# A hybrid two-layer kernel on Trainium2: the maxima of causal attention computed for two heads at a time on 64 rows each

## The chip, the cores and the metric

The kernel runs on one core of one Trainium2 chip. A time is the device time of one execution in microseconds (us); "before" is the median of three runs. Next to it stands one execution recorded by the hardware profiler. Times inside that execution are counted from the start of its span. The engines are TensorE (PE in the profile; its weight loads are PEld), VectorE (DVE), ScalarE (ACT), GpSimd (POOL) and SyncE (SP), which here only issues DMAs.

## The reference, cut to what matters

The reference is two layers of several sublayers each, with a residual sum around each: a complex-valued scan (`sublayer_a`), a routed feed-forward, a second attention-like sublayer and the same feed-forward, then a long convolution (`sublayer_c`), a ternary feed-forward, causal self-attention (`sublayer_d`) and the ternary feed-forward again. The change touches only the causal attention, on x of shape (2, 2048, 256), with 16 heads of 16 features:

```python
q, k, v = (proj(Wq), proj(Wk), proj(Wv))        # (B, heads, S, 16)
q = _apply_rope(q, cos, sin)
k = _apply_rope(k, cos, sin)
scores = jnp.einsum('bhqd,bhkd->bhqk', q, k) * scale      # scale = 1/4
scores = jnp.where(causal[None, None], scores, -jnp.inf)
attn = jax.nn.softmax(scores, axis=-1)
out = jnp.einsum('bhqk,bhkd->bhqd', attn, v)
out = out.transpose(0, 2, 1, 3).reshape(B, S, 256)
return jnp.einsum('bsd,ed->bse', out, Wo)
```

The softmax subtracts the maximum of each row of scores before the exponential.

## The kernel before

`tile_hybrid_kernel` calls the sublayers one after the other. `sublayer_d` first calls `attention_inputs`, which writes q, k (each as a high and a low part[...]) and v to device memory (`qd`, `kd`, `vd`). Then it works in units. A unit is one batch `b`, one group `g` of four heads and one chunk `ch` of 512 queries; it needs the keys of chunks 0 to `ch`. There are 2 x 4 x 4 = 32 units, four of them (`ch` 0 to 3) in each of the eight groups.

`load_unit` (L1446 and after) fills a tile `d_kt` (six of them in turn) and a tile `d_qt` (three in turn) for a unit. `stack` (L1439) does it with four DMAs for each: the features of a head lie four times over on 64 partitions, as high and low parts in the orders that make a product of 64 rows the sum of all four high-low combinations. Rows 64 and 65 of `d_kt` are ones. Rows 64 and 65 of `d_qt` are set to zero by GpSimd (L1459) and later take the negative row maxima as a high and a low part, and all other rows to 127 are zero. So a product over 128 partitions gives the scores before the maxima are known, and the scores less the maxima afterwards.

`maxima` (L1463) makes the row maxima of a unit. For each head `hh`, block `i` of 128 queries and key chunk `j` it makes a product into a `ps_m` buffer (L1472; three buffers of 128 x 512) and reduces it on VectorE: with `tensor_reduce` (L1482), or, on the diagonal chunk, with an added mask row (L1477). The results stand in `d_part`; at the end they are reduced to `d_mx` (L1485), transposed by TensorE into the single buffer `ps_x` (L1489), split (L1491, L1492) and sent into rows 64 and 65 of `d_qt` by two DMAs on ScalarE's queue. It is a generator that yields after each product.

`attend` (L1497) runs over the key tiles `kt` of 128 keys. For each of four heads it makes the transposed scores into a `ps_e` buffer (L1515; three buffers); on the diagonal it adds the causal mask with a second product (L1520: `d_mask` times `d_identr`). ScalarE takes the exponential into a `d_p` buffer (L1522; six buffers), and then `filler` may let the next unit's `maxima` go on. When the four heads of a key tile are issued, the value products of the key tile before it follow (`values`, L1503), into four strips of 32 partitions of `ps_o`; `v` has ones appended, so that the sums of the softmax come out too. At the end ScalarE copies `ps_o` to `d_on` (L1531), and the sums are turned over by three DMAs of GpSimd's queue around a reciprocal on VectorE (L1535). `normalize` and `project` (L1549) finish the unit one step later: products with `Wo` into `ps_x` (L1554), added to `self.x` by VectorE (L1559).

In the loop at the end of `sublayer_d` step `n` runs `attend` of unit `n` with `maxima` of unit `n + 1` in between, spread over the first 70% of the key tiles, and issues the loads of unit `n + 2`:

```python
filler(1.0)
if late is not None:
    project(*late)
late = (unit, on)
```

TensorE's instructions run in the order in which this code writes them (`tc.manual_schedule(engines={PE})`). The order on the other engines is decided when the kernel is compiled, by a scheduler that works with its own estimate of times; on the chip each engine keeps that order.

Of the kernel before, what the change touches and what calls it, by code (L numbers as in the profile page):

```python
# [16 lines left out]
F32 = mybir.dt.float32  # L17
# [46 lines left out]
class Kernel:  # L64
# [1320 lines left out]
    def sublayer_d(self):  # L1385
# [5 lines left out]

        tc, nc = self.tc, self.nc
# [3 lines left out]
        with ExitStack() as c:  # L1396
# [8 lines left out]
            mask, identr = r32(kp, [P, P], "d_mask"), r32(kp, [P, P], "d_identr")  # L1405
            V.tensor_copy(mask, maskf)
            V.tensor_copy(identr, self.ident)
# [18 lines left out]
            qring = [r32(qp, [P, 4, CH], f"d_qt{j}") for j in range(QR)]  # L1426
            for t in qring:
                G.memset(flat(t, HR, P), 0.0)
# [3 lines left out]
            sp = c.enter_context(tc.tile_pool(name="d_s", bufs=6))  # L1432
            pm = c.enter_context(tc.tile_pool(name="d_pm", bufs=3, space=PSUM))
            pe = c.enter_context(tc.tile_pool(name="d_pe", bufs=3, space=PSUM))
            po = c.enter_context(tc.tile_pool(name="d_po", bufs=1, space=PSUM))
            px = c.enter_context(tc.tile_pool(name="d_px", bufs=1, space=PSUM))
            wo = self.load(kp, "D_WoP", pat="(k p) n -> p k n", p=P)

            def stack(t, src, b, g, blk, order):  # L1439
                for r, half in enumerate(order):  # L1440
# [3 lines left out]
                    )  # L1444

            def load_unit(b, g, ch):  # L1446
# [8 lines left out]
                stack(kring[(n * 4 + ch) % KR], kd, b, g, ch, (0, 0, 1, 1))  # L1455
                q = qring[(n * 4 + ch) % QR]
                stack(q, qd, b, g, ch, (0, 1, 0, 1))
                if n * 4 + ch >= QR:
                    G.memset(flat(q, HR, ROWS), 0.0)  # L1459
                ks = [kring[(n * 4 + j) % KR] for j in range(ch + 1)]  # L1460
                return b, g, ch, q, ks, vring[n % 2]

            def maxima(unit):  # L1463

                b, g, ch, q, ks, ve = unit
                part = new(tp, [P, 4, 4, 4], "d_part")
                for hh in range(4):
                    for i in range(4):
                        for j in range(ch + 1):
                            w = (i + 1) * P if j == ch else CH  # L1470
                            ps = new(pm, [P, CH], "ps_m")
                            nc.tensor.matmul(  # L1472
                                ps[:, :w], q[:, hh, i * P : (i + 1) * P], ks[j][:, hh, :w], start=True, stop=True
                            )
                            if j == ch:
                                junk = new(jp, [P, CH], "d_junk")
                                V.tensor_tensor_reduce(  # L1477
                                    out=junk[:, :w], in0=ps[:, :w], in1=late_keys[:, CH - w :], scale=1.0,
# [16 lines left out]
                yield  # L1495

            def attend(unit, o, filler):  # L1497
                b, g, ch, q, ks, ve = unit
                nk = 4 * ch + 4

                def values(kt, q0, prs):
# [196 lines left out]
```

## Time and profile before

| | us |
|---|---|
| median of three runs | 13912.62 (13908.2 to 13919.0) |
| the profiled execution | 13913.98 |
| its span, first to last instruction | 13912.3 |
| busy in the span: DVE | 10663.1 (77%) |
| busy in the span: ACT | 9306.1 (67%) |
| busy in the span: PE | 5521.0 (40%) |
| units of `sublayer_d` in the span | 12322 to 13756 |
| in this stretch: PE, DVE, ACT busy | 1254.9, 762.0, 624.4 |
| in this stretch: granted TensorE clock | 0.96 |

The busy shares of the whole span are those of the scan, which takes about the first 10000 us and keeps TensorE mostly idle. A row of a group gives the line, the engine, the operation and the tiles (written first), then the count, the time in which at least one of them ran, the mean duration in ns, and the idle time of the engine just before them with what ended it. Matmul durations overlap: the pace is in the distance from one start to the next. In the timeline, a bracket at the end of a row gives the idle time before it and what ended it.

### The profile page before, as it was taken

To read this page: it belongs to the slowest core of one execution; us is meant where nothing else is said; L and a number is where in the kernel's file an instruction comes from. 1 tells how busy PE (TensorE), PEld (TensorE's weight loads), DVE (VectorE), ACT (ScalarE), POOL (GpSimd) and SP (SyncE) were. 2 spreads that over 40 slices of the span, in tenths; PEclk is the share of its full clock that TensorE was granted. 3 is DMA by queue.
4 is the path that set the end of the run, shared out by engine and by line. 5 is a ranking of instruction groups with operands and counts; after the bars stand their busy time and mean duration, and the time that the engine had idled before them with its cause. 6 is when DMAs were issued, how large, how long until landed. Compare 5 with 4: busy or idle time off the path is not lost. (4 is left out here: it accounts for less than half of the span.)

```text
span 13912.3 us, 263001 instructions
## 1 busy us (share of the span) xinstructions
PE 5521.0 (40%) x66344; PEld 3798.1 (27%) x66344; DVE 10663.1 (77%) x65491; ACT 9306.1 (67%) x45234; POOL 432.4 (3%) x496
## 2 busy tenths in 40 slices
PE   4222222222222222222222222222289766778888
PEld 2111111111111111111111111111255444544445
DVE  6888888888888888888888888888857655555555
ACT  3777777777777777777777777777626366434444
POOL 0000000000000000000000000000000000131110
PEclk7555555555555555555555555555579778889999
DMA  3000000000000000000000000000000144242210
GB/s 80 14 15 16 17 14 17 14 17 17 14 17 14 17 17 14 17 14 17 17 14 17 14 17 17 14 17 14 14 13 1 41 123 132 62 94 35 33 32 19
DMA packets 334776, 382.28 MB, mean 27 GB/s; under 512 B 207074, under 2 KB 247081, under 8 KB 332212
## 3 DMA queue, kind: packets, MB, share of 16 engines
q1 hardware_dynamic: 289204, 281.11, 8.8%
q10 hardware_dynamic: 29184, 49.82, 1.3%
q0 software_dynamic: 14848, 34.36, 0.9%
q8 instruction: 533, 8.73, 0.3%
q14 instruction: 1007, 8.25, 0.2%
HBM read 307.96 MB, written 52.46 MB: 26 GB/s over the span
## 5 line engine op out<-in xcount | busy, mean ns | idle before, releaser
L410 PE MATMUL hc<-hs,mean 128*32 128x2 f32 x16384 | 588.2, 203 | 7116.8 <-DVE hs L480 7052.2
L410 PEld LDWEIGHTS hc<-hs,mean 128*32 128x32 f32 x16384 | 412.7, 140 | 7328.8 <-DVE hs L480 7263.8
L475 DVE TENSOR_TENSOR p<-p,ir 128x64 f32<-128x64 f32 x4096 | 739.0, 222 | 1065.4 <-ACT ir L463 1065.4
L459 ACT ACTIVATE lm<-m 128x64 f32<-128x64 f32 x2048 | 466.2, 228 | 1216.3 <-DVE m L451 1216.3
L493 PE MATMUL yps<-cs,hist 128*64 128x8 f32 x8192 | 1225.0, 259 | 13.0 <-DVE hs L480 13.0
L391 ACT ACTIVATE bx<-dx,tc 128x64 f32<-128x64 f32 x4098 | 1169.4, 332 | 0.1
L1522 ACT ACTIVATE d_p<-ps_e 128x512 f32<-128x512 f32 (+3 forms) x1280 | 599.4, 537 | 756.1 <-PE ps_o L1503 534.2
L493 PEld LDWEIGHTS yps<-cs,hist 128*64 128x64 f32 x8192 | 1033.2, 218 | 45.1 <-DVE hs L480 13.4
L418 ACT ACTIVATE sq<-hc 128x2 f32<-128x2 f32 x2048 | 353.2, 172 | 794.0 <-PE hc L410 794.0
L480 DVE CUSTOM_DVE_ANT_0 hist<-p,sg 128x64 f32<-128x64 f32 x4096 | 764.5, 224 | 22.5 <-ACT rm L470 4.2
L442 DVE TENSOR_TENSOR p<-p,fac 128x64 f32<-128x64 f32 x4096 | 741.6, 222 | 8.9 <-DVE p L437 6.6
L477 DVE SCALAR_TENSOR_TENSOR p<-e,p 128x64 f32<-128x64 f32 x4096 | 740.6, 222 | 9.9 <-ACT sg L469 7.8
L444 DVE TENSOR_TENSOR p<-p,bx 128x64 f32<-128x64 f32 x4096 | 727.5, 219 | 2.5
L439 ACT ACTIVATE fac<-ngd,ci 128x64 f32<-128x64 f32 x2048 | 711.8, 348 | 1.0 <-DVE p L436 1.0
L436 DVE SCALAR_TENSOR_TENSOR p<-hist,ea 128x64 f32<-128x64 f32 x2048 | 461.1, 225 | 321.8 <-ACT ea L429 321.8
L429 ACT ACTIVATE ea<-ex 128x64 f32<-128x64 f32 x2048 | 524.3, 256 | 102.7 <-DVE ex L424 7.0
L1515 PE MATMUL ps_e<-d_qt,d_kt 128*128 128x512 f32 (+3 forms) x1280 | 558.1, 445 | 44.3 <-ACT d_p L1522 35.5
L472 ACT ACTIVATE ld<-e 128x64 f32<-128x64 f32 x2048 | 548.2, 268 | 0.0
L410 PE MATMUL hd<-hs,mean 128*32 128x2 f32 x16384 | 544.3, 193 | 0.0
L473 ACT ACTIVATE k<-rm 128x64 f32<-128x64 f32 x2048 | 544.1, 266 | 0.0
L1472 PE MATMUL ps_m<-d_kt,d_qt 128*128 128x512 f32 (+3 forms) x1280 | 499.9, 438 | 99.1 <-DVE d_part L1477 39.9
L1165 PE MATMUL ps_c<-toep,c_x 128*32 128x128 f32 x9216 | 407.5, 341 | 306.6 <-ACT toep L1114 304.9
(452 smaller groups left out, 22795.9 us busy)
## 6 DMA issues: line engine op xcount, KB each, us to landing
ng<-dtd SPq DMA_DIRECT2D x258, 256.0 KB, 3.7
dx<-dxd SPq DMA_DIRECT2D x258, 256.0 KB, 4.2
toep<-in_C_krev ACTq DMA_DIRECT2D x128, 312.0 KB, 4.7
toep<-in_C_krev SPq DMA_DIRECT2D x128, 312.0 KB, 4.7
d_kt<-d_kd SPq DMA_DIRECT2D x128, 128.0 KB, 4.1
d_qt<-d_qd SPq DMA_DIRECT2D x128, 128.0 KB, 3.8
y<-ys SPq DMA_DIRECT2D x512, 8.0 KB, 1.9
c_xd<-c_xs POOLq DMA_DIRECT2D x32, 256.0 KB, 4.5
```

The source lines that it names most:

```text
L391: A.activation(bx[o][:, k2], tg[j][2][:, k], AF.Identity, scale=tg[j][0][:, k2, k : k + 1], bias=0.0 if k2 else SMALL,)
L410: nc.tensor.matmul(out[r : r + 32], mean[:, r : r + 32], hs[i], start=True, stop=True)
L439: A.activation(fac, ngd, AF.Exp, scale=ci)
L442: V.tensor_tensor(p[:, k2], p[:, k2], fac, ALU.mult)
L444: V.tensor_tensor(p[:, k2], p[:, k2], bx[o][:, k2], ALU.add)
L472: A.activation(ld, e, AF.Ln, scale=-1.0, bias=1.0)
L475: V.tensor_tensor(p[:, k2], p[:, k2], ir, ALU.mult)
L477: V.scalar_tensor_tensor(p[:, k2], e, -1.0, p[:, k2], ALU.add, ALU.mult)
L480: V.tensor_tensor_reduce(out=hn[:, k2], in0=p[:, k2], in1=sg, scale=-1.0, scalar=0.0 if k2 else J * SMALL, op0=ALU.mult, op1=ALU.add, accu ...
L493: nc.tensor.matmul(yps[:, k, :], hist[g][:, k, k2], tg[g][3][:, k2, k], start=k2 == 0, stop=k2 == 1)
L1515: nc.tensor.matmul(s[:, q0:], ks[kt // 4][:, hh, kt % 4 * P : (kt % 4 + 1) * P], q[:, hh, q0:], start=True, stop=not diag,)
L1522: A.activation(pr[:, q0:], s[:, q0:], AF.Exp, scale=0.25)
```

## The change

The products for the maxima are made for two heads at a time. The even head uses rows 0 to 63 of `d_qt` and `d_kt`, as they are; the odd head uses rows 64 to 127 of new tiles `d_qq` (two in turn) and `d_kk` (five in turn), which a DMA inside SBUF copies from rows 0 to 63 of the odd heads. Each product thus takes 64 of TensorE's rows, and the two of a pair go to different rows and different `ps_m` buffers. `maxima` yields once per pair. The rows 64 and 65 of `d_qt` are no longer read before the maxima are in them, and the memset of them goes. The mask and the identity that adds it are bfloat16. The pool of `ps_x` goes; its users take a `ps_m` buffer, and there are four of these instead of three. There are eight `d_p` buffers instead of six.

```diff
@@ -1402,9 +1404,9 @@
             kp = c.enter_context(tc.tile_pool(name="d_k", bufs=1))
             maskf = new(kp, [P, P], "d_maskf")
             make_causal_mask(nc, maskf, MASKED)
-            mask, identr = r32(kp, [P, P], "d_mask"), r32(kp, [P, P], "d_identr")
+            mask, identb = (kp.tile([P, P], BF16, name=n, tag=n) for n in ("d_mask", "d_identb"))
             V.tensor_copy(mask, maskf)
-            V.tensor_copy(identr, self.ident)
+            V.tensor_copy(identb, self.ident)
 
             late_keys = new(kp, [P, CH], "d_late")
             G.memset(late_keys, 0.0)
@@ -1424,24 +1426,26 @@
             self.attention_inputs(qd, kd, vd)
             qp = c.enter_context(tc.tile_pool(name="d_q", bufs=1))
             qring = [r32(qp, [P, 4, CH], f"d_qt{j}") for j in range(QR)]
+            q2ring = [r32(qp, [P, 2, CH], f"d_qq{j}") for j in range(2)]
+            k2ring = [r32(qp, [P, 2, CH], f"d_kk{j}") for j in range(5)]
             for t in qring:
                 G.memset(flat(t, HR, P), 0.0)
             tp = c.enter_context(tc.tile_pool(name="d_t", bufs=2))
             jp = c.enter_context(tc.tile_pool(name="d_j", bufs=1))
             op = c.enter_context(tc.tile_pool(name="d_o", bufs=3))
-            sp = c.enter_context(tc.tile_pool(name="d_s", bufs=6))
-            pm = c.enter_context(tc.tile_pool(name="d_pm", bufs=3, space=PSUM))
+            sp = c.enter_context(tc.tile_pool(name="d_s", bufs=8))
+            pm = c.enter_context(tc.tile_pool(name="d_pm", bufs=4, space=PSUM))
             pe = c.enter_context(tc.tile_pool(name="d_pe", bufs=3, space=PSUM))
             po = c.enter_context(tc.tile_pool(name="d_po", bufs=1, space=PSUM))
-            px = c.enter_context(tc.tile_pool(name="d_px", bufs=1, space=PSUM))
             wo = self.load(kp, "D_WoP", pat="(k p) n -> p k n", p=P)
 
-            def stack(t, src, b, g, blk, order):
+            def stack(t, t2, src, b, g, blk, order):
                 for r, half in enumerate(order):
                     nc.sync.dma_start(
                         out=t[r * 16 : (r + 1) * 16].bitcast(F32),
                         in_=src[b, g * 4 : g * 4 + 4, half, :, blk * CH : (blk + 1) * CH].rearrange("h c t -> c h t"),
                     )
+                nc.sync.dma_start(out=t2[HR:P].bitcast(F32), in_=t[0:HR, 1::2].bitcast(F32))
 
             def load_unit(b, g, ch):
                 n = b * 4 + g
@@ -1452,40 +1456,41 @@
                             out=vring[n % 2][:, :, hh, 0:16],
                             in_=vd[b * S : (b + 1) * S, h * 16 : (h + 1) * 16].rearrange("(i p) e -> p i e", p=P),
                         )
-                stack(kring[(n * 4 + ch) % KR], kd, b, g, ch, (0, 0, 1, 1))
-                q = qring[(n * 4 + ch) % QR]
-                stack(q, qd, b, g, ch, (0, 1, 0, 1))
-                if n * 4 + ch >= QR:
-                    G.memset(flat(q, HR, ROWS), 0.0)
-                ks = [kring[(n * 4 + j) % KR] for j in range(ch + 1)]
-                return b, g, ch, q, ks, vring[n % 2]
+                u = n * 4 + ch
+                stack(kring[u % KR], k2ring[u % 5], kd, b, g, ch, (0, 0, 1, 1))
+                q, q2 = qring[u % QR], q2ring[u % 2]
+                stack(q, q2, qd, b, g, ch, (0, 1, 0, 1))
+                ks, k2s = ([ring[(n * 4 + j) % len(ring)] for j in range(ch + 1)] for ring in (kring, k2ring))
+                return b, g, ch, q, ks, vring[n % 2], q2, k2s
 
             def maxima(unit):
 
-                b, g, ch, q, ks, ve = unit
+                b, g, ch, q, ks, ve, q2, k2s = unit
                 part = new(tp, [P, 4, 4, 4], "d_part")
-                for hh in range(4):
+                for hp in range(2):
                     for i in range(4):
                         for j in range(ch + 1):
                             w = (i + 1) * P if j == ch else CH
-                            ps = new(pm, [P, CH], "ps_m")
-                            nc.tensor.matmul(
-                                ps[:, :w], q[:, hh, i * P : (i + 1) * P], ks[j][:, hh, :w], start=True, stop=True
-                            )
-                            if j == ch:
-                                junk = new(jp, [P, CH], "d_junk")
-                                V.tensor_tensor_reduce(
-                                    out=junk[:, :w], in0=ps[:, :w], in1=late_keys[:, CH - w :], scale=1.0,
-                                    scalar=MASKED, op0=ALU.add, op1=ALU.max, accum_out=part[:, hh, i, j : j + 1],
-                                )
-                            else:
-                                V.tensor_reduce(part[:, hh, i, j : j + 1], ps[:, :w], AX.X, ALU.max)
+                            two = [new(pm, [P, CH], "ps_m") for _ in range(2)]
+                            for ps, qs, kt in (
+                                (two[0], q[0:HR, 2 * hp], ks[j][0:HR, 2 * hp]), (two[1], q2[HR:P, hp], k2s[j][HR:P, hp]),
+                            ):
+                                nc.tensor.matmul(ps[:, :w], qs[:, i * P : (i + 1) * P], kt[:, :w], start=True, stop=True)
+                            for hh, ps in enumerate(two, 2 * hp):
+                                if j == ch:
+                                    junk = new(jp, [P, CH], "d_junk")
+                                    V.tensor_tensor_reduce(
+                                        out=junk[:, :w], in0=ps[:, :w], in1=late_keys[:, CH - w :], scale=1.0,
+                                        scalar=MASKED, op0=ALU.add, op1=ALU.max, accum_out=part[:, hh, i, j : j + 1],
+                                    )
+                                else:
+                                    V.tensor_reduce(part[:, hh, i, j : j + 1], ps[:, :w], AX.X, ALU.max)
                             yield
                 mx = new(tp, [P, 16], "d_mx")
                 V.tensor_reduce(
                     mx, part[:, :, :, : ch + 1].rearrange("p h i j -> p (h i) j"), AX.X, ALU.max, negate=True
                 )
-                ps = new(px, [P, CH], "ps_x")
+                ps = new(pm, [P, CH], "ps_m")
                 nc.tensor.transpose(ps[:16, :P], mx, self.ident)
                 hi, lo = r32(tp, [16, P], "d_mhi"), r32(tp, [16, P], "d_mlo")
                 A.copy(hi, ps[:16, :P])
@@ -1495,7 +1500,7 @@
                 yield
 
             def attend(unit, o, filler):
-                b, g, ch, q, ks, ve = unit
+                b, g, ch, q, ks, ve = unit[:6]
                 nk = 4 * ch + 4
 
                 def values(kt, q0, prs):
@@ -1517,7 +1522,7 @@
                             start=True, stop=not diag,
                         )
                         if diag:
-                            nc.tensor.matmul(s[:, q0 : q0 + P], mask, identr, start=False, stop=True)
+                            nc.tensor.matmul(s[:, q0 : q0 + P], mask, identb, start=False, stop=True)
                         pr = new(sp, [P, CH], "d_p")
                         A.activation(pr[:, q0:], s[:, q0:], AF.Exp, scale=0.25)
                         prs.append(pr)
@@ -1549,7 +1554,7 @@
             def project(unit, on):
                 b, g, ch = unit[:3]
                 for i0 in range(0, 4, 2):
-                    ps = new(px, [P, CH], "ps_x")
+                    ps = new(pm, [P, CH], "ps_m")
                     for i in (i0, i0 + 1):
                         nc.tensor.matmul(
                             ps[:, (i - i0) * D : (i - i0 + 1) * D], on[:, i * P : (i + 1) * P], wo[:, g, :],
@@ -1571,7 +1576,7 @@
                 unit = units[n]
                 todo, total, done = None, 0, 0
                 if n + 1 < len(keys):
-                    todo, total = maxima(units[n + 1]), 16 * (keys[n + 1][2] + 1) + 1
+                    todo, total = maxima(units[n + 1]), 8 * (keys[n + 1][2] + 1) + 1
                 if n + 2 < len(keys):
                     units.append(load_unit(*keys[n + 2]))
                 state = [0]
```

## The prediction

> **What bounds the kernel now.** I read the 40 slices of the page first: the attention part (`sublayer_d`) lies near the end, from 12322 to about 13756 us of the span, where TensorE is busiest. Everything before and after it is untouched. Then I cut one of its eight groups (four steps; a step ends when ScalarE copies `ps_o` to `d_on`) into its steps with the table of stretches:
>
> ```profile
> core 0: us, PE busy (x) PEld busy (x) DVE busy (x) ACT busy (x) POOL busy (x), PEclk, DMA share, GB/s
> 12684.50:12712.90 28.40, 22.17 (x106) 14.80 (x105) 18.58 (x53) 7.18 (x18) 6.74 (x9) 0.88 0.48 65
> 12712.90:12754.00 41.10, 35.94 (x170) 19.37 (x169) 28.33 (x69) 15.67 (x34) 6.75 (x9) 0.96 0.12 21
> 12754.00:12807.60 53.60, 49.60 (x235) 24.07 (x234) 37.97 (x85) 23.57 (x51) 6.76 (x9) 1.00 0.09 17
> 12807.60:12859.80 52.20, 47.61 (x234) 19.74 (x233) 9.88 (x37) 31.49 (x66) 6.75 (x9) 1.00 0.27 47
> ```
>
> Call them steps 0 to 3: attention of key chunk `ch` runs beside the maxima of the next unit. The other groups repeat these lengths within a few per cent, so a group is 175.3 us and eight are 1402. In steps 0 to 2 VectorE does 32, 48 and 64 maxima; in step 3 only 16 small ones, and there neither VectorE (9.9) nor ScalarE (31.5) is full. The groups of the whole part give the unit costs:
>
> ```profile
> L1482 DVE TENSOR_REDUCE d_part<-ps_m 128x1 f32<-128x512 f32 x768 | 495.0, 683 | 40.4 <-PE ps_m L1472 39.7
> L1522 ACT ACTIVATE d_p<-ps_e 128x512 f32<-128x512 f32 x896 | 474.7, 602 | 590.9 <-PE ps_o L1503 392.1 <-PE ps_e L1515 110.2 <-PE ps_e L1520 68.3
> L1515 PE MATMUL ps_e<-d_qt,d_kt 128*128 128x512 f32 x896 | 422.5, 476 | 27.9 <-ACT d_p L1522 22.3 <-DMA d_qt<-d_mlo 3.9
> L1472 PE MATMUL ps_m<-d_kt,d_qt 128*128 128x512 f32 x896 | 396.2, 475 | 59.2 <-DVE d_part L1477 25.5 <-DVE d_part L1482 22.3
> ```
>
> The first releaser on the L1522 row is the surprise: ScalarE's exponentials wait for the value products (`ps_o`), because a `d_p` buffer is free only when they have read it. The list of waits over the part has it at the top for ScalarE:
>
> ```profile
> ACT d_p L1522 <- PE ps_o L1503: 534.2, 287, 4.9
> DVE d_rs L1535 <- DMA d_rs<-d_sd: 55.2, 31, 4.0
> PEld ps_x L1554 <- DVE x L1559: 38.1, 32, 1.5
> ```
>
> The timeline of step 3 shows how that sets the pace (one key tile `kt`: four `ps_e`, four exponentials, one block of value products):
>
> ```profile
> 12840.67 0.19 PEld L1515 LDWEIGHTS ps_e<-d_qt,d_kt 128*128 128x128 f32 x1 [0.84 <-issue]
> 12840.82 2.07 ACT L1522 ACTIVATE d_p<-ps_e 128x512 f32<-128x512 f32 x4 [1.37 <-PE ps_o L1503]
> 12841.47 0.19 PEld L1515 LDWEIGHTS ps_e<-d_qt,d_kt 128*128 128x128 f32 x1 [0.61 <-ACT d_p L1522]
> 12842.45 0.19 PEld L1515 LDWEIGHTS ps_e<-d_qt,d_kt 128*128 128x128 f32 x1 [0.31 <-ACT d_p L1522]
> 12842.88 0.16 PEld L1503 LDWEIGHTS ps_o<-d_p,d_ve 128*32 128x32 f32 x8 [0.24 <-issue]
> 12843.88 0.19 PEld L1515 LDWEIGHTS ps_e<-d_qt,d_kt 128*128 128x128 f32 x1 [0.84 <-issue]
> 12844.02 2.06 ACT L1522 ACTIVATE d_p<-ps_e 128x512 f32<-128x512 f32 x4 [1.14 <-PE ps_o L1503]
> ```
>
> The reader is to see a ring of 3.20 us (12840.82 to 12844.02). With six `d_p` buffers, exponentials 2 and 3 of a key tile wait until the values of the tile before are done; then three exponentials (0.49 apart, the last 0.60) free the `ps_e` buffer of the fourth score product, that starts 0.05 later (12842.45), the values follow 0.43 after it and take 1.07.
>
> In steps 1 and 2 VectorE is the bound with a hole at each value block:
>
> ```profile
> 12766.94 1.89 DVE L1482 TENSOR_REDUCE d_part<-ps_m 128x1 f32<-128x512 f32 x3 [0.45 <-PE ps_m L1472]
> 12771.77 1.89 DVE L1482 TENSOR_REDUCE d_part<-ps_m 128x1 f32<-128x512 f32 x3 [0.60 <-PE ps_m L1472]
> 12776.37 0.69 DVE L1477 CUSTOM_DVE_ANT_0 d_junk<-ps_m,d_late 128x512 f32<-128x512 f32 x1 [0.44 <-PE ps_m L1472]
> ```
>
> **The change part by part.** VectorE's work is unchanged: 1280 maxima, 0.62 us from start to start for a full one (1.88 for three), about 0.41 for a diagonal one (0.21, 0.33, 0.47, 0.62 by width). So halving TensorE's share cannot by itself halve anything.
>
> *Eight `d_p` buffers in place of six* (the edit that the description doesn't name). Exponentials no longer wait for the values of the tile before. New ring from the end of exponential 0: the fourth score product at 0.05, values at 0.48, next score product 1.00 later (12842.88 to 12843.88), its exponential 0.54 after that (0.43 is seen from a score matmul's start to its exponential with the weights loaded ahead, 12761.87 to 12762.30, and 0.11 more for an exposed load), 0.60 for the exponential: 2.63. ScalarE alone needs 4 x 0.49 = 1.96. Gain 0.57 per key tile; in step 3 thirteen full tiles give 7.4, the three narrower ones about 1.2 together, and eight pairs now put into the ring cost about 0.8 more than the sixteen single products did: -7.8 us. The last tiles of steps 1 and 2 have the same ring, over 2 and 3 tiles: -1.0 and -2.0. Step 0 ends on VectorE: nothing.
>
> *No `px` pool; `project` and the transpose take `ps_m` buffers, four in all.* The second pair of `project` products waited 1.18 for VectorE's addition each step (the third line of the waits). Now both pairs run at once, and the first score product comes 1.3 earlier in each step. In step 3 that is 1.3 off. In steps 0 to 2 VectorE soon stands at the reciprocal `d_rs` for its chain of DMAs (it comes 8.9, 6.6 and 6.1 us after the copy of `d_on` in steps 0, 1, 2), which doesn't move; the compiled order leaves 7, 3 and 4 maxima ahead of it (5, 3 and 2 before).
>
> *Pairs on 64 rows.* Every score product is 128 rows, the pair 64, the values 32 columns[...]. The trace shows three such changes. From a score product to the values 0.43 passes, where 0.34 is its own (0.11 exposed load, 0.23 stream): 0.09 for the change. After the values the load is exposed: 0.11. In `scan_tables`, transposes of 128 rows followed by a product of 64 (L224, 264.76, to L215, 265.11) are 0.35 apart instead of 0.21, at half the clock. So a score product costs 0.34 + 0.09 and a pair 0.34 + 0.09: 0.86, four of them and the values (1.00) 4.44 us. [...] I take the trace's 0.09, as the value block's load does begin 0.07 before that recorded end. For the two halves running together no 64-row pair is in the trace; the four value products of one block, in column strips, start 7 ns apart. [...]a pair is one stream, 0.23. If they ran one after the other: 0.45.
>
> *VectorE's order.* It is compiled ahead. In the changed kernel the second half of each diagonal pair stands behind the first half of the next pair. A value block comes after every fourth pair in step 2, which is just after a diagonal pair. Then: the diagonal pair issues when the pair two back is reduced (t); values end at t + 1.43; a score product 0.43; the next pair's first tile is readable 0.55 later, t + 2.4. VectorE has 1.25 + 0.41 of work and then must wait 0.7. Eight maxima take 6 x 0.627 + 2 x 0.41 = 4.58 + 0.7 = 5.28 us against 4.99 now (64 of them in 40). TensorE's 4.44 fits below it, with 0.2 to spare per pair.
>
> Sums of VectorE's stages, from the `d_on` copy. Step 0: reciprocal done 9.05, 25 tiles at 0.52, 1.0 of stalls, then 3.5 + 0.6 as now: 27.5 against 28.4. Step 1: 6.75 + 24.7 + 2.1 = 33.6 against 34.4, 38.4 to the end against 41.1 after the ring's 1.0 and the later start of the tail. Step 2: 6.25 + 34.2 + 4.4 = 44.9 against 42.7, less 2.0 in the ring and 1.3 in overlap of the last tiles: 52.6 against 53.6. Step 3: -7.8 - 1.3 = -9.1. Together -13.7 per group, -110 in all.
>
> *Copies, memsets, mask.* 64 copies of 256 KB inside SBUF go on SP's queue; each waits there until the four loads before it have landed (4.1 and 3.8 us), and the next loads queue behind it. By the compiled order each copy is through about three quarters of a step (20 us or more) before its maxima begin; only the first unit has no cover: +4 us once. With no cover each unit would pay 12. The 29 memsets of `d_qt` leave POOL (52 us of an idle engine: nothing); they stood ahead of the `d_sd` chain but had ended before it. Masks in bfloat16: a load of 0.10 (L1304) instead of 0.19, mostly hidden, same 0.11 stream: nothing, at most 512 x 0.09 = 46 us if every load were exposed.
>
> Sum: 13914.0 (the profiled execution; span 13912.3; the median of the three runs is 13912.6) - 110 + 4 = **13808**.
>
> **The rivals.** [...]
>
> *Half the ring.* The three `ps_e` buffers or the pairs hold the score products and the ring is 2.9: 13860. 17 in 100.
>
> *No holes.* VectorE never waits at the swap, and steps 0 to 2 save 7.5 more per group: 13748. 12 in 100.
>
> *Not concurrent.* The pairs run in turn at cheap changes: 0.23 more per pair, about the slack: 13825. It is inside the main case.
>
> **How the numbers follow.** Main case 55 in 100, 13770 to 13845. Between it and no change (the 0.2%, 28 us, that a measurement of this kernel can tell) lies half the ring[...]. Range 13735 to 13890. Faster 0.83, same 0.06, slower 0.11.
>
> **What would show it.** Step 3 near 43 us, ScalarE's wait for `ps_o` almost gone and key tiles 2.6 apart; the wait of `ps_x` for `x` gone; pairs of `ps_m` starting within 0.15 of each other where both buffers are free; steps 0 to 2 within 3 us of now, VectorE waiting 0.7 at value blocks that follow a diagonal pair. It is wrong if a score product behind a pair starts over 0.6 after it, or if step 3 stays above 48.

## The result, and the profile after

The change made the kernel slower: 14025.6 us (median of four runs, 14008.0 to 14035.3) against 13911.9 us for the kernel before on the same chip. The ratio is 1.0079, with a 95% interval of 1.0066 to 1.0092. The prediction was 13808 us (13735 to 13890), faster; the change went the other way.

The steps of one group, cut as before at ScalarE's copy into `d_on` (the columns are stretch, length, busy time of each engine, granted TensorE clock, DMA share, GB/s), in the changed kernel:

```profile
core 0: us, PE busy (x) PEld busy (x) DVE busy (x) ACT busy (x) POOL busy (x), PEclk, DMA share, GB/s
12725.80:12757.70 31.90, 27.81 (x106) 14.44 (x106) 18.84 (x53) 7.56 (x18) 4.94 (x8) 0.63 0.47 70
12757.70:12811.20 53.50, 47.30 (x170) 19.77 (x171) 29.14 (x69) 16.66 (x35) 4.94 (x8) 0.65 0.21 37
12811.20:12870.20 59.00, 55.43 (x234) 23.72 (x233) 38.30 (x85) 26.04 (x51) 4.96 (x8) 0.91 0.12 24
12870.20:12913.00 42.80, 41.30 (x234) 17.35 (x233) 9.97 (x37) 31.60 (x66) 4.95 (x8) 1.00 0.33 60
```

Step 3 fell from 52.2 to 42.8 us, as forecast (43.1). Steps 0 to 2 grew by 3.5, 12.4 and 5.4 us where they should have shrunk. VectorE and ScalarE have nearly the busy time that they had. What differs is the column before the last two: the clock granted to TensorE is 0.63, 0.65 and 0.91, where it was 0.88, 0.96 and 1.00. In step 3 it is 1.00 in both kernels.

Over the whole attention part, from the first to the last `d_on` copy, the same view of the kernel before gives the first row and of the changed kernel the second:

```profile
12359.30:13733.90 1374.60, 1220.12 (x5791) 607.54 (x5792) 730.02 (x1863) 615.70 (x1326) 203.94 (x276) 0.97 0.20 32
12376.70:13843.80 1467.10, 1352.77 (x5791) 586.84 (x5792) 741.48 (x1863) 646.64 (x1325) 153.37 (x248) 0.81 0.23 40
```

The clock has two values in these records, 1 and 0.5. A mean of 0.97 is thus about (1 - 0.97) x 2 x 1374.6 = 82 us at half clock, and 0.81 is about 557 us; the half-clock spells in the records add up to 89 and 570 us. TensorE's busy time rose by 133 us, with the same number of products.

The waits that the prediction named, in the list of waits of the changed kernel (engine, what waits, for what: total us, times, longest):

```profile
ACT d_p L1527 <- PE ps_e L1520: 479.3, 467, 6.2
ACT d_p L1527 <- PE ps_e L1525: 326.3, 234, 6.3
DVE d_part L1487 <- PE ps_m L1478: 171.7, 153, 4.5
DVE d_rs L1540 <- DMA d_rs<-d_sd: 92.5, 32, 4.7
```

ScalarE's wait for `ps_o` (534 us before) has fallen to 2.5 us, and the projection's wait for `x` is gone from the list. Now ScalarE waits for score products (110.2 and 68.3 us before for the same two products) and VectorE for the products of the maxima (39.7 us before): both wait for a slower TensorE. The timeline of step 3 has the new ring, 2.60 us from key tile to key tile, with the values 1.08 behind the first exponential (2.63 had been forecast):

```profile
12895.99 2.06 ACT L1527 ACTIVATE d_p<-ps_e 128x512 f32<-128x512 f32 x4 [0.69 <-PE ps_e L1520]
12897.07 1.06 PE L1508 MATMUL ps_o<-d_p,d_ve 128*32 128x512 f32 x8
12898.59 1.58 ACT L1527 ACTIVATE d_p<-ps_e 128x512 f32<-128x512 f32 x3 [0.54 <-PE ps_e L1520]
```

One way in which the clock is lost is seen in the timeline of step 2:

```profile
12813.05 0.49 PE L1478 MATMUL ps_m<-d_kt,d_qt 64*128 64x512 f32 x1
12813.05 0.49 PE L1478 MATMUL ps_m<-d_kk,d_qq 64*128 64x512 f32 x1
12813.47 0.50 PE L1520 MATMUL ps_e<-d_qt,d_kt 128*128 128x512 f32 x1
12813.91 0.50 PE L1478 MATMUL ps_m<-d_kt,d_qt 64*128 64x512 f32 x1
...
12819.26 0.25 DVE L1540 RECIPROCAL d_rs<-d_rs 128x16 f32<-128x16 f32 x1 [3.21 <-DMA d_rs<-d_sd]
12820.12 0.53 PE L1478 MATMUL ps_m<-d_kt,d_qt 64*128 64x512 f32 x1 [3.25 <-DVE d_part L1487]
...
12822.15 0.79 PE L1478 MATMUL ps_m<-d_kt,d_qt 64*128 64x512 f32 x1
12822.16 0.79 PE L1478 MATMUL ps_m<-d_kk,d_qq 64*128 64x512 f32 x1
12822.88 0.79 PE L1520 MATMUL ps_e<-d_qt,d_kt 128*128 128x512 f32 x1
12823.60 0.79 PE L1478 MATMUL ps_m<-d_kt,d_qt 64*128 64x512 f32 x1
```

At the top the two halves of a pair start together, the score product follows after 0.42 and the next pair after 0.44: 0.86 us, the prediction's figure. Then VectorE stands 3.21 us at the reciprocal, with its reductions queued behind it; the next pair finds no free `ps_m` buffer and TensorE stands 3.25 us. From there on a product is recorded with 0.79 in place of 0.50, and a score product and a pair take 1.45 us. While the clock is low, TensorE is the bound. In this step it is back after 6.8 us; in steps 0 and 1 of the same group the half-clock spells last 23.9 and 37.5 us. The kernel before loses its clock in such places too; in this part it always has it back after 3.4 or 6.8 us.

A wait is not needed for a loss. Later in the same step a whole stretch of 3.41 us at full clock shows TensorE busy without a gap, and the next stretch is at half clock:

```profile
12854.58:12857.99 3.41, 3.41 (x13) 1.63 (x16) 3.41 (x8) 1.79 (x3) 0.00 (x0) 1.00 0.36 77
12857.99:12861.41 3.42, 3.42 (x13) 1.00 (x5) 2.04 (x6) 0.78 (x2) 0.00 (x0) 0.50 0.03 7
```

Records of products overlap, so this is not TensorE at its peak; but it does not stand still. Three score products run in the first of the two stretches (for 1.17 us, one of them only in part) and value products for 0.19 us; products on 64 rows fill the rest.

### The profile page after: what moved, and what is told of

Its sections match the earlier page's. It is cut to its first block, busy times and chain, and to the rows that moved or that the text cites. A ratio compares the mean times of both kernels' runs of the same rounds, so it can differ in the third digit from the quotient of the medians.

```text
span 14020.7 us, 262688 instructions
## 1 busy us (share of the span) xinstructions
PE 5685.2 (41%) x66344; PEld 3795.8 (27%) x66344; DVE 10656.9 (76%) x65491; ACT 9328.5 (67%) x45234; POOL 380.1 (3%) x467
## 5 line engine op out<-in xcount | busy, mean ns | idle before, releaser
L1527 ACT ACTIVATE d_p<-ps_e 128x512 f32<-128x512 f32 (+3 forms) x1280 | 632.9, 535 | 822.0 <-PE ps_e L1520 479.3
L1487 DVE TENSOR_REDUCE d_part<-ps_m 128x1 f32<-128x512 f32 x768 | 493.6, 683 | 172.5 <-PE ps_m L1478 171.7
L1520 PE MATMUL ps_e<-d_qt,d_kt 128*128 128x512 f32 (+3 forms) x1280 | 597.7, 508 | 31.7 <-ACT d_p L1527 20.0
```

The costliest lines, as they stand in the source:

```text
L1520: nc.tensor.matmul(s[:, q0:], ks[kt // 4][:, hh, kt % 4 * P : (kt % 4 + 1) * P], q[:, hh, q0:], start=True, stop=not diag,)
L1527: A.activation(pr[:, q0:], s[:, q0:], AF.Exp, scale=0.25)
```

## The experiments

The theory to test (theory 1): the wait at `d_rs` starts a loss of clock that the kernel has always had, and the pairs put too little on TensorE's array for the clock to come back. Rivals: the changes between 64-row and 128-row products cost the time (1), a 64-row product counts as little activity by itself (2), the other edits do it (3), or standing still is what counts, whatever is done in between (4). In the end rival 2 turned out to be the sharper form of theory 1.

All results, with the ratio to the kernel before on the same chip; the attention part is measured from the first to the last `d_on` copy, and the steps are means over the groups of the profiled execution:

| kernel | median us | ratio (95%) | attention us, clock | steps 0, 1, 2, 3 us |
|---|---|---|---|---|
| before | 13912 | 1 | 1374.6, 0.97 | 28.3, 41.1, 53.8, 52.2 |
| changed | 14025.6 | 1.0079 (1.0066 to 1.0092) | 1467.1, 0.81 | 32.1, 50.5, 61.9, 42.9 |
| all but the pairs | 13777.1 | 0.9892 (0.9875 to 0.9908) | 1227.1, 0.95 | 25.2, 39.0, 49.5, 42.7 |
| 96 rows, single | 13790.7 | 0.9915 (0.9899 to 0.9932) | 1244.3, 0.93 | 26.9, 39.3, 50.0, 42.7 |
| 64 rows, single | 14266.5 | 1.0242 (1.0225 to 1.0260) | 1712.5, 0.68 | 32.2, 59.2, 82.5, 44.2 |
| pairs twice | 14006.8 | 1.0056 (1.0039 to 1.0073) | 1448.2, 0.89 | 33.0, 49.4, 58.9, 43.8 |
| scores twice | 14004.5 | 1.0063 (1.0046 to 1.0079) | 1448.3, 0.88 | 32.5, 48.5, 61.2, 42.9 |
| pairs, late reciprocal | 13903.6 | 0.9986 (0.9979 to 0.9993) | 1358.2, 0.84 | 28.9, 46.1, 55.4, 43.0 |
| pairs, late reciprocal, VectorE in order | 13878.8 | 0.9969 (0.9958 to 0.9980) | 1344.0, 0.82 | 27.7, 44.7, 56.2, 42.9 |
| pairs, late reciprocal, 24 useless products | 13866.6 | 0.9966 (0.9954 to 0.9979) | 1316.7, 0.89 | 30.3, 41.2, 54.1, 42.8 |
| pairs, late reciprocal, 32 useless products | 13850.4 | 0.9955 (0.9939 to 0.9972) | 1327.2, 0.90 | 26.7, 41.4, 58.3, 42.8 |
| eight `d_p` only | 13848.8 | 0.9950 (0.9933 to 0.9966) | 1300.8, 0.96 | 27.4, 41.5, 53.3, 43.9 |
| no `px`, four `ps_m` only | 13843.4 | 0.9945 (0.9929 to 0.9962) | 1297.2, 0.97 | 25.8, 38.5, 50.0, 51.2 |
| all but the pairs, late reciprocal | **13704.7** | **0.9846 (0.9830 to 0.9863)** | 1155.8, 1.00 | 22.1, 35.7, 46.8, 42.7 |

**All edits but the pairs.** The kernel before with these edits (shortened):

```diff
-sp = tile_pool(name="d_s", bufs=6)
+sp = tile_pool(name="d_s", bufs=8)
-pm = tile_pool(name="d_pm", bufs=3, space=PSUM)
-px = tile_pool(name="d_px", bufs=1, space=PSUM)
+pm = tile_pool(name="d_pm", bufs=4, space=PSUM)     # transpose and project take ps_m
-mask, identr = r32(...), r32(...)
+mask, identb = (kp.tile([P, P], BF16, ...) ...)
```

> All edits of the change but the pairs: eight `d_p` buffers, four `ps_m` and no `px`, the mask in bfloat16; the maxima keep their 128-row products, one head at a time, and there are no copies. Theory 1 (the pairs leave TensorE with so little streaming that its granted clock, once lost at the wait for `d_rs`, does not come back through steps 0 to 2): the clock of steps 0 to 2 stays as in the kernel before (0.88, 0.96, 1.00), step 3 is 42 to 45 us against 52.2, the other steps within 2 us of the kernel before, and the time is near 13820 us (13790 to 13850). Rival 1 (changes between 64-row and 128-row products cost time as such): the same numbers here. Rival 3 (the other edits bring TensorE earlier to the wait and make the low clock): clock of steps 0 and 1 below 0.75, time 13950 us or more.

Its time is 13777.1 us, better than any theory said; the steps of a group, in the table of stretches:

```profile
12820.60:12846.30 25.70, 20.28 (x106) 12.69 (x106) 18.42 (x53) 7.64 (x18) 7.61 (x10) 0.87 0.56 73
12846.30:12885.60 39.30, 33.47 (x170) 18.44 (x171) 28.20 (x69) 16.76 (x35) 5.88 (x9) 0.96 0.20 29
12885.60:12935.20 49.60, 45.74 (x234) 24.90 (x234) 37.94 (x85) 25.70 (x50) 6.68 (x10) 0.97 0.09 17
```

The clock is 0.87, 0.96 and 0.97 with the wait still there (77.7 us at `d_rs` in all). Rival 3 falls. What slows the changed kernel lies in the pairs and what comes with them (the copies, the memset that goes): the ratios 1.0079 and 0.9892 are 1.9% apart, 260 us, and the attention parts differ by 240 us. The place of the loss is the same in both. By the clock records, the half-clock spells in this group begin 8.6, 10.2 and 8.5 us into steps 0 to 2 and last 6.8, 3.4 and 3.4 us. In a group of the changed kernel (from 12913.0) they begin 9.8, 5.4 and 8.5 us in, and last 20.5, 23.9 and 17.1.

**64 rows, one head at a time.** From the kernel without pairs:

```diff
-ps[:, :w], q[:, hh, i * P : (i + 1) * P], ks[j][:, hh, :w], start=True, stop=True
+ps[:, :w], q[0:HR, hh, i * P : (i + 1) * P], ks[j][0:HR, hh, :w], start=True, stop=True
-G.memset(flat(q, HR, ROWS), 0.0)
```

> As the kernel with all edits but the pairs, but each product for the maxima uses the lower 64 rows alone, one head at a time: as many products and as many streamed columns as on 128 rows, and as many changes between 64-row and 128-row products as the changed kernel has or more. The zero fill of the query tiles' upper rows is left out. Theory 1 (it is the streaming time that counts): clock of steps 0 to 2 within 0.05 of the kernel with all edits but the pairs, time within 40 us of it. Rival 1 (each change of form costs time as such, some 0.1 to 0.2 us): at full clock the score product and the single maximum product together take 1.0 to 1.3 us in place of 0.86, and the time is 60 us or more above it, clock unchanged. Rival 2 (a product on 64 rows counts as half the activity for the clock): clock of steps 0 and 1 below 0.75, time 13950 us or more.

```profile
12776.00:12808.60 32.60, 29.36 (x106) 16.29 (x107) 19.00 (x53) 7.65 (x19) 4.94 (x8) 0.64 0.43 59
12808.60:12870.20 61.60, 57.03 (x170) 25.14 (x171) 29.76 (x69) 17.05 (x35) 4.94 (x8) 0.58 0.13 18
12870.20:12953.20 83.00, 81.10 (x234) 32.23 (x234) 40.33 (x85) 26.09 (x51) 4.95 (x8) 0.59 0.06 11
12953.20:12997.70 44.50, 43.92 (x234) 18.97 (x234) 9.99 (x37) 31.71 (x67) 4.95 (x8) 1.00 0.28 49
```

This is the run that says most. There are as many products, columns and score products as without pairs, TensorE is busy for nearly the whole of each step, and yet the clock is 0.64, 0.58 and 0.59: 14266.5 us. There are no copies in it, so they are not needed for the loss. A half-clock spell fills most of step 2, with TensorE busy for 67.55 of 68.27 us:

```profile
12877.60:12945.87 68.27, 67.55 (x154) 24.76 (x154) 35.87 (x76) 18.52 (x31) 3.80 (x6) 0.50 0.02 5
```

So the clock did not go with the time in which TensorE streams, as theory 1 first had it: on 128 rows TensorE was busy for 45.7 of the 49.6 us of step 2 at 0.97, on 64 rows for 81.1 of 83.0 us at 0.59. What differs between the two kernels is the rows of these products, with the changes of form around them. As a cost in time, it is also not the change of form (rival 1): step 3 mixes 64-row and 128-row products at full clock, and costs 44.5 us against 42.8 for its 16 products for the maxima, about 0.1 us each. One rival stays untested: every kernel here with 64-row products also has changes of form around them, so what these changes do to the clock cannot be told apart from what the fewer rows do. They are not enough by themselves, since in the runs below added products bring the clock up (0.89 and 0.88 over the attention part against 0.81) with as many changes as before.

**96 rows, one head at a time.** As the last, with `q[0:96, ...]` and `ks[j][0:96, ...]`, the memset kept.

> All edits but the pairs, with the products for the maxima on the lower 96 rows alone, one head at a time (rows 66 to 95 hold zeros in the query tiles, so that nothing is left out of the sums). On 128 rows the clock of steps 0 to 2 was 0.88, 0.93, 0.96 and the time 13777 us, on 64 rows 0.64, 0.60, 0.59 and 14266 us; waits, order and columns are the same in the three. If the clock follows the share of rows that work, half-clock spells last longer than on 128 rows and shorter than on 64: clocks between the two, time 13830 to 14150 us. If any product on less than all rows counts as on 64, or if the change of form is what matters, time above 14200 us. If only half the array or less counts as idle, within 40 us of 13777 us.

```profile
12812.70:12840.20 27.50, 22.09 (x106) 13.19 (x106) 18.44 (x53) 7.64 (x19) 7.60 (x10) 0.81 0.51 69
12840.20:12880.40 40.20, 33.71 (x170) 19.09 (x171) 28.20 (x69) 16.70 (x34) 5.83 (x9) 0.92 0.19 28
12880.40:12930.90 50.50, 46.67 (x234) 25.52 (x234) 37.94 (x85) 25.75 (x51) 6.77 (x10) 0.93 0.09 17
```

The time, 13790.7 us, is within 40 us of the one on 128 rows, as the last case had it. The clocks of steps 0 to 2 do lie below those on 128 rows, by little, and the spells last 6.8 to 10.2 us in steps 0 and 1. The dose is ordered (128, 96, 64 rows: about 123, 174 and 1096 us at half clock, from the clock and the length of the attention part) and far from linear. Most of the rise, from about 174 to 1096 us, lies between 96 and 64 rows; what lies between them was not tried.

**Each pair twice, and each score product twice.** The first repeats the pair (`) * 2:` behind the two operands). The second is

```diff
+for last in (False, True) if ch < 3 else (True,):
     nc.tensor.matmul(s[:, q0:], ks[kt // 4][...], q[:, hh, q0:],
-                     start=True, stop=not diag)
+                     start=True, stop=not (diag and last))
```

> The changed kernel with each pair of products issued twice into the same two buffers: TensorE streams as many columns for the maxima as before the change. Theory 1: although work is added, the clock of steps 0 to 2 comes back (0.85 or more over the three, against 0.63, 0.65 and 0.91 in the changed kernel), and the time falls under the changed kernel's, to 13830 to 13980 us; step 3, where the clock was full, gets longer than its 42.8 us by up to 32 times 0.43 us if TensorE sets it, by less where VectorE does. Rival 1 (changes of form are the cost): no change of form is taken away, so that 640 further pairs of 0.43 us come on top of TensorE's chain: 14100 to 14300 us.

> The changed kernel with each score product of the steps 0 to 2 (all 128 rows, into `ps_e`) issued twice, the second overwriting the first: 96 useless full-array products in each group of four steps, 768 in all, of about 0.34 us. Nothing waits less and no change of form goes away. Theory 1, as the 64-row run has sharpened it (the clock follows how much of the array works: a 64-row product counts half or less): the clock of steps 0 to 2 is 0.93 or more in place of 0.64, 0.70 and 0.84, the steps take 26 to 29, 39 to 44 and 50 to 55 us in place of 32.1, 50.5 and 61.9, and the time falls to 13780 to 13880 us in spite of the added work. Rival 1 (changes of form, or the pairs' own time): the added products come on top, 96 x 0.34 x 8 = 261 us: 14200 us or more. Rival 4 (what counts is that TensorE stands still at VectorE's waits, not how much it does between them): the clock stays under 0.85 and the time is 14050 us or more.

In both kernels the clock comes back some way (0.89 and 0.88 against 0.81). By the medians both are slightly faster than the changed kernel (14006.8 and 14004.5), but the intervals of the ratios overlap with its own; what is shown is that 1280 and 768 products done for nothing cost no time. Both miss my time, and the second also its clock (0.71, 0.84 and 0.92 in steps 0 to 2 in place of 0.93 or more). I had not summed TensorE's chain: at full clock step 2 has 48 score products and 32 pairs of about 0.43 us and 12 value blocks of 1.0, 46 us, and the useless work adds 14 to 16 us there. What the clock gave, the longer chain took, as far as this sum goes. So they speak for the clock and against rivals 1 and 4, but not cleanly.

**Pairs with a late reciprocal.** In the changed kernel, `normalize` (with the reciprocal now in it) moves from ahead of `attend` into its middle:

```diff
-    V.reciprocal(rs, rs)                       # end of attend
-    G.dma_start(out=sd[n, 1]..., in_=rs)
+    # both at the head of normalize
+    if kt == nk // 2 - 1:
+        midway()                               # normalize of the unit before
```

> The changed kernel with the reciprocal of `d_rs`, the DMA behind it and the normalizing (four DMAs and the GpSimd multiply) emitted in the middle of the next step in place of before it, so that VectorE does not stand at `d_rs` and TensorE does not stand behind it. Theory 1 (this wait is what starts each loss of the clock): VectorE's waits at the reciprocal fall from 92.5 us to under 20, the clock of the attention part rises from 0.79 to 0.90 or more, and the time falls to 13780 to 13880 us. Rival 1 (changes of form): the clock and the time stay within 50 us of the changed kernel's. Rival 2 (the little activity of the pairs itself keeps the clock low, whatever starts it): the waits go and the clock stays below 0.85, time above 13930 us.

```profile
13029.10:13058.70 29.60, 28.16 (x106) 14.84 (x107) 18.89 (x53) 7.61 (x19) 4.94 (x8) 0.63 0.46 70
13058.70:13106.70 48.00, 45.46 (x170) 19.33 (x171) 29.14 (x69) 16.61 (x34) 4.94 (x8) 0.68 0.23 41
13106.70:13158.40 51.70, 51.41 (x234) 22.84 (x234) 38.05 (x85) 25.79 (x50) 4.95 (x8) 1.00 0.14 27
```

VectorE's wait at `d_rs` falls from 92.5 to 20.1 us and 122 us are saved (129 by the ratios), but the clock still goes, some 8 us into each step 0, with no long wait ahead of it. The time, 13903.6 us, lies between theory 1's and rival 2's; the clock, 0.84 in place of 0.90 or more, is rival 2's. The wait is not the only thing that starts a loss: theory 1 was too narrow in this.

**The same with fewer useless products, in steps 0 and 1 alone.** `for last in (False, True) if ch < 2 and hh % 2 == 0 else (True,)` makes 24 a group; `ch < (1, 2)[hh % 2 == 0]` makes 32, the further 8 all in step 0.

> The changed kernel with the late reciprocal, and in steps 0 and 1 every second score product (128 rows) issued twice, the second overwriting the first: 24 useless full-array products in each group. With the late reciprocal alone the clock was lost some 8 us into each step 0 and 6 us into each step 1, with no long wait ahead of it, and stayed away 10 to 20 us: steps of 28.9, 46.1, 55.4 and 43.0 us. At full clock TensorE's chain with the added products would be some 20 us in step 0 (16 x 0.43 + 8 x 0.34 + 16 pairs x 0.43 + 4 value blocks) and 37 us in step 1, under VectorE's 21 and 32 to 37 us. Theory 1 (too little of the array works ahead of each loss, and the clock does not come back for the same reason): the spells in steps 0 and 1 become rare or short, clock 0.9 or more, steps of 22 to 25, 37 to 41, 52 to 54 and 43 us, and the time is 13750 to 13830 us although work is added. Without that effect the clocks stay at 0.64 and 0.72 and the added 8.2 us a group make 13900 us or more. In either case it stays above the kernel with single products and the late reciprocal (13705 us), if the pairs have no gain at full clock.

> As the kernel that issues every second score product of steps 0 and 1 twice, but in step 0 every score product twice (16 in place of 8 useless products there). With 8, step 1 had come to a clock of 0.89 and step 0 had not moved: its clock went some 6.7 us into the step in five of seven groups, behind a window of 3.4 us in which the score products streamed for 0.22 of the time and the 64-row products for 0.39 (both halves added), and stayed away for 23.9 us. Theory 1: the further products lift such windows to some 0.4 for full-array work alone, step 0 keeps its clock (0.9 or more) and takes 22 to 26 us in place of 30.3, and the time falls by 35 to 70 us, to 13800 to 13830 us. If the clock of step 0 does not hang on the full-array work, step 0 keeps 0.64 and gets longer by up to 8 x 0.68 us, and the time rises by 10 to 45 us.

The first two steps with 24, then the first two with 32:

```profile
12677.30:12708.10 30.80, 29.31 (x114) 16.18 (x114) 18.88 (x53) 7.63 (x19) 4.94 (x8) 0.61 0.46 72
12708.10:12750.00 41.90, 40.78 (x186) 19.07 (x187) 29.04 (x69) 16.77 (x35) 4.95 (x8) 0.88 0.26 47
```

```profile
13037.90:13062.20 24.30, 22.20 (x122) 12.85 (x122) 18.71 (x53) 7.64 (x19) 4.95 (x8) 1.00 0.65 99
13062.20:13104.70 42.50, 40.81 (x186) 18.96 (x187) 29.05 (x69) 16.76 (x34) 4.96 (x8) 0.88 0.25 42
```

With 24, step 1 goes from 46.1 to 41.2 us with 16 products more in it, and step 0 keeps its low clock (30.3 us after 28.9); the time, 13866.6 us, lies between the two that were forecast. With 8 more in step 0, its mean falls from 30.3 to 26.7 us and its mean clock rises from 0.64 to 0.88, just short of the forecast. Work that nobody needs, on all rows, makes the step shorter. The median of the whole time fell by 16 us, less than the 35 to 70 expected and within the intervals of the two ratios. A reason is seen in the trace: in the profiled execution of the last kernel (13889.6 us, above its median of 13850.4) step 2, in which nothing was added, took 58.3 us in the mean in place of 54.1; in the group of the second table its clock was 0.71, in that of the first 1.00.

**VectorE in the written order.** The late reciprocal, and `manual_schedule(engines={PE, DVE})`.

> The changed kernel with the late reciprocal, and in addition VectorE kept to the order in which its instructions are written, so that both halves of a diagonal pair are reduced one behind the other. It is to tell what the pairs cost where the clock is full: there a step 2 took 51.7 us with pairs and 46.8 us with single products on 128 rows. If VectorE's swapped order is the cause (5.28 us for 8 maxima in place of 4.99, and a wait of 0.7 at each value block behind a diagonal pair), steps 2 at full clock fall to 47.5 to 49.5 us and the time lies 15 to 40 us under the kernel with the late reciprocal alone. If it is TensorE's chain (48 score products and 32 pairs of some 0.43 us and 12 value blocks of 1.0 make 46 us) or the waits that come with two buffers taken at once, steps 2 at full clock stay above 50.5 us. The low clock of steps 0 and 1 stays in either case, 0.6 to 0.8.

It is to tell what pairs cost where the clock is full. With the compiled order the timeline of a full-clock step 2 of the kernel with the late reciprocal has VectorE's waits at 5.2 to 5.4 us from one to the next, as the prediction drew them (5.28 and 0.7):

```profile
13117.98 0.69 DVE L1487 TENSOR_REDUCE d_part<-ps_m 128x1 f32<-128x512 f32 x1 [0.79 <-PE ps_m L1478]
13123.20 0.69 DVE L1487 TENSOR_REDUCE d_part<-ps_m 128x1 f32<-128x512 f32 x1 [0.72 <-PE ps_m L1478]
13128.60 0.69 DVE L1487 TENSOR_REDUCE d_part<-ps_m 128x1 f32<-128x512 f32 x1 [0.64 <-PE ps_m L1478]
```

In the written order the list of waits for such a step has 0.6 us of them in place of 4.1, and the step takes 49.8 us in place of 51.7:

```profile
12568.30:12618.10 49.80, 49.49 (x234) 22.15 (x234) 38.52 (x85) 25.80 (x51) 4.96 (x8) 1.00 0.14 28
```

The whole time is 25 us under that with the compiled order, as expected of the order, though the intervals of the two ratios just touch; the step is just above the range for the order as the whole cause. Single 128-row products do a step 2 in 46.8. So at full clock the order is worth 1.9 of the 4.9 us (seen in the one step 2 of this run that was at full clock throughout), and 3.0 us remain. In both rows TensorE is busy for all but 0.3 us, so its own chain is the likely owner, but no run separated it.

**Eight `d_p` alone; no `px` and four `ps_m` alone.** One part each of the first diff, on the kernel before.

> The kernel before with eight `d_p` buffers in place of six, nothing else. The kernel with all edits but the pairs gained 146 us on the kernel before, more than the 110 that the prediction gave to the whole change. If the wider key-tile ring alone carries what the prediction gave it (7.8 us in step 3, 2.0 in step 2, 1.0 in step 1 of each of 8 groups), the time is 80 to 90 us under the kernel before and step 3 is near 44 us. If the ring needs the freed PSUM bank as well, step 3 stays above 48 us.

> The kernel before with four `ps_m` buffers and no `px` pool (transpose and projection take `ps_m`), nothing else. The prediction gave this 1.3 us at the head of each step, 4 steps in 8 groups: 42 us. If the fourth maximum buffer also keeps VectorE from waiting in steps 1 and 2, 50 to 70 us; if the effects of the ring and of this overlap, the two kernels' gains add up to more than the 146 us of both together, if each needs the other, to less. Step 3 stays at 50 us or more in either case.

By the ratios they save 0.50% and 0.55%, 70 and 76 us; together with the mask, 1.08%. They simply add, and what is left for the mask is far below the intervals. The first is nearly all step 3 (52.2 to 43.9). The second is 1.0 us in step 3 and 2.5, 2.6 and 3.8 in steps 0 to 2, where VectorE's wait of `d_part` for `ps_m` falls from 39.7 to 16.8 us.

**All edits but the pairs, with the late reciprocal.**

> All edits of the change but the pairs, and the reciprocal of `d_rs` with the normalizing in the middle of the next step. In the changed kernel the late reciprocal alone took 122 us away. [...]VectorE's waits at the reciprocal before the move are some 2 to 3 us in each of 32 steps. Theory 1: 40 to 90 us under the kernel with all edits but the pairs, 13690 to 13740 us, with the clock of step 0 near 1.00. If VectorE only meets its next wait sooner, within 20 us of that kernel.

```profile
12784.40:12806.30 21.90, 19.57 (x105) 11.14 (x105) 18.07 (x53) 7.66 (x18) 6.44 (x10) 1.00 0.65 87
12806.30:12843.30 37.00, 34.09 (x170) 18.46 (x171) 28.12 (x69) 16.73 (x34) 6.96 (x10) 0.95 0.20 31
12843.30:12890.40 47.10, 45.44 (x234) 23.97 (x235) 37.69 (x85) 25.77 (x51) 6.85 (x10) 1.00 0.10 19
12890.40:12933.10 42.70, 41.50 (x234) 18.52 (x233) 9.86 (x37) 31.33 (x67) 6.70 (x10) 1.00 0.31 51
```

13704.7 us, the best of all: 1.5% under the kernel before, and by the ratios 64 us under the kernel with all edits but the pairs, where theory 1 had 40 to 90. Here the same move that only shifted the loss with pairs removes it: the clock of the attention part is 1.00 after rounding, and the wait at `d_rs` is 13.1 us in all.

## Why the prediction was wrong, point by point

- *Eight `d_p` buffers.* Right in step 3: alone they gain 8.3 us there, where the term without its 0.8 for the pairs makes 8.6, and the ring is 2.60 us against 2.63. That step as a whole came out as forecast (42.8 us against 43.1); its clock is full in both kernels. The 1.0 and 2.0 us at the ends of steps 1 and 2 were not seen with this edit alone (41.1 to 41.5 and 53.8 to 53.3).
- *No `px` pool.* Right in step 3 (1.0 against 1.3), and the mechanism of `project` was right. It was too small for steps 0 to 2: I put 1.3 us there on the score products and left VectorE's end fixed by the reciprocal. The fourth `ps_m` buffer also cuts VectorE's waits later in the step, and the edit is worth 76 us where the term made 42.
- *Pairs on 64 rows.* The price at full clock was right to the hundredth: 0.86 us for a score product and a pair, both halves starting together. *Not concurrent* is refuted by the same rows, and so is a change of rows that costs more than that at full clock. The sign of being wrong that I had named, more than 0.6 us from a pair to the score product behind it, did come (0.72), but at half clock; at full clock it was 0.42. And "a score product costs 0.34 + 0.09 and a pair 0.34 + 0.09" is a price at full clock, and that was taken for granted.
- *The failed step.* It is the sums of steps 0 to 2, "27.5", "38.4", "52.6": all their TensorE terms assume that the clock stays as it was, although the table of stretches that I showed had 0.88 and 0.96 in steps 0 and 1. It fell to 0.63, 0.65 and 0.91. A score product and a pair at half clock take 1.45 us, more than VectorE's two reductions (2 x 0.62), so that TensorE becomes the bound. The group shown went from 175.3 to 187.2 us in place of 161.6. No rival had the clock as its mechanism. That TensorE, which bounded none of these steps, could be given less to do at no cost was never questioned, and it was false. Where the clock stayed full, the sum was not far off: two steps 2 with pairs and a late reciprocal took 51.7 us against the 52.6 forecast for the reciprocal in its old place.
- *Two sums.* As written, the terms of step 0 give 9.05 + 25 x 0.52 + 1.0 + 3.5 + 0.6 = 27.2 us and not 27.5, and of the 2.7 us that step 1 was to gain only 0.8 + 1.0 are accounted for. Neither changes the outcome.
- *VectorE's order.* Right as drawn (waits of 0.64 to 0.79 us, 5.2 to 5.4 us for eight maxima at full clock), and worth 1.9 us of a full-clock step 2. In steps 0 and 1, which lose their clock with either order, the written order is 1.2 and 1.4 us shorter (28.9 to 27.7, 46.1 to 44.7).
- *Copies, memsets, mask.* No cost to be seen of mask and memsets, as said. The copies were not tried alone; in the waits of the changed kernel TensorE stands for one of them once, for 2.9 us, near the 4 us once that was forecast.

## What to carry to other kernels

Look at the granted clock of each stretch before you take work off TensorE: where it is below 1, price the change at both clocks (here 0.86 and 1.45 us for a score product and a pair), and ask how the clock comes back after a wait, not only how it is lost. In these runs, with one head at a time, the clock of the attention part was 0.68 with products on 64 rows, 0.93 on 96 and 0.95 on 128, and packing work denser on an engine that bounds nothing made it the bound. The cheap gains were elsewhere: more buffers where an engine waits, and a reciprocal moved to where its DMA has long landed.

## What the runs showed of the hardware that I had not expected

- In the trace of the kernel before, the attention part has 17 half-clock spells of 3.41 or 6.83 us; in that of the changed kernel it has 37, of 3.41 to 40.96 us. All of these lengths are multiples of 3.41 us.
- A busy TensorE did not by itself go with a full clock: with single 64-row products it was busy for 81.1 of 83.0 us of a step and the clock was 0.59; with 128 rows, for 45.7 of 49.6 us at 0.97.
- In the kernel before, TensorE was busy for 0.09 to 0.69 of the 3.41 us ahead of each of the 17 spells, and for 0.97 or more of the last 3.41 us of each. In the changed kernel the busy share ahead of a spell says less: in 13 of the 37 cases it was 0.95 or more. These are counts of two traces, and no run tested what decides.
